# Layer 1's queries by head: two of the four masked copies moved from ScalarE to GpSimd

## The chip, the cores and the metric

The kernel runs on one core of a Trainium2 chip, in one launch. The metric is the device time of a run in microseconds (us). The engines are called as in the profile: PE is TensorE's matmul, PEld its weight load, ACT is ScalarE, DVE is VectorE, POOL is GpSimd, SP is SyncE. Times inside a run are counted from the start of the profiled span.

## The reference, cut to what matters

Four layers work on x of shape 4 x 1024 x 128. Each has a modulated layer norm, an attention, a second norm and a feed-forward part. The change lies in layer 1's attention alone, which itself has four sublayers of causal linear attention with 16 heads of 8 columns, on chunks of 128 positions:

```python
q = elu(x @ Wq[l] + bq[l]) + 1      # k likewise, v without the elu
KV = einsum('bnchd,bnche->bnhde', k, v)
KVcum = cumsum(KV, axis=1) - KV
inter = einsum('bnchd,bnhde->bnche', q, KVcum)
scores = einsum('bnchd,bnkhd->bnhck', q, k)
scores = where(tril, scores, 0.0)
intra = einsum('bnhck,bnkhe->bnche', scores, v)
out = (inter + intra) / (den_inter + den_intra + 1e-6)
x = ln(x + out @ Wo[l] + bo[l]);  y = gelu(x @ W1[l] + b1[l]) @ W2[l] + b2[l];  x = ln(x + y)
```

## The kernel before

**Stages.** Layer 0 is a program part of its own (`l0`). Layers 1 to 3 are one part (`rest`, L2056), in which some thirty chains of work run interleaved. Layer 1's attention (`l1_attn`, L892) takes the four sublayers l and the eight steps n of 128 positions (all four batches at once, so tiles are 128 x 512), which makes 32 steps.

**What sets the order.** Each chain is a Python generator. It yields requests: `run(ACT=..., POOL=...)` with a cost in us for each engine, `take(kind)` for a buffer, `wait(mark)` for another chain's mark, `rank(r)` for its precedence. The planner `Flow` (L120 to L209) keeps a clock for each engine and always goes on with the chain that can start first, or with one of lower rank that can start within 0.1 us of it. When a `run` is granted, each engine named in it has its clock set to the later of its own clock and the chain's time, plus the cost; the chain goes on at the latest of these ends. The instructions that follow in the generator are emitted at that point. PE, DVE, ACT and POOL then execute in just the emitted order (`in_order`, L483), each its own queue, and wait for each other by semaphores. The planner's costs are thus no times on the chip, but they fix the order on four engines.

**A step of layer 1.** `prep` runs in two chains, three ranks ahead. `prep_step` (L932 to L1032) makes:

- q and k: a matmul each (line L304, the helper `mm`), `min` of the biased value on DVE (L943), `relu` on ACT (L944), the exponential of both on ACT (L953), and the sum of the two on POOL (L956);
- v on DVE (L961), k transposed (PE L968, ACT L970), the running sum of k (DVE L985 to L992), and the denominator's reciprocal `rd` (DVE L1003, L1004), which POOL widens to `rde` (L1008) and PE (L1014) and ACT (L1017) turn into `rb`;
- last, **qx** and **vz**. PE works on groups of 32 rows, which hold four heads. `qx` holds q four times, the s-th copy kept only where the row belongs to the s-th head of its group: ACT multiplies q by a column of zeros and ones (L1024, four times 128 x 512). `vz` spreads v over a tile of zeros (POOL L1027, four copies). Both have two buffers. Then the mark `aprep` is set.

Around it:

- `scores` (L1039) multiplies k with qx on PE (L304, out `three` and one more bank), in two pairs of batches;
- `mask_dve` (L1066) masks three of four banks on DVE (L1073); `mask_act` (L1081) copies the fourth out on ACT (L1089) and masks it on POOL (L1093);
- `state` (L1097) makes the chunk's k v product, masked on DVE (L1116) and added up on POOL (L1122, L1124), into `kvb` and `kv`;
- `values` (L1129) multiplies q with kv and kvb (PE L1145), then vz with the masked scores (PE L1163, many small matmuls);
- `attn_out` (L1173) divides (DVE L1182) and projects (DVE L1190);
- `tail` (two chains) does the norms and the feed-forward with four gelus (ACT L1212). A norm (`norm`, L506) goes PE L514, ACT L517, DVE L523 and L525, POOL L527 and L528, DVE L531, PE L539, ACT L543 or L547.

The planner reckons a POOL operation on 512 columns at `pool_len(512)` = 0.2 + 0.0021 * 512 = 1.28 us, and one qx on ACT at 0.72 us.

## Time and profile before

| | before |
|---|---|
| median of 3 runs | 1982.12 us (1981.19 to 1982.89) |
| profiled execution, own time | 1977.38 us |
| its span in the profile | 1975.6 us |
| mean granted TensorE clock | 0.974 |
| PE, DVE, ACT, POOL busy in the span | 1802.3, 1200.7, 1033.8, 774.7 us |
| layer 1's qx: ACT L1024 | 128 instructions, 82.0 us busy |
| layer 1's vz: POOL L1027 | 128 instructions, 32.2 us busy |

The profiled execution lies 4.74 us under the median of the runs and 3.81 us under the fastest of them; 1.78 us of its own time lie outside the span. A row of busy tenths has one digit for each fortieth of the span, 49.4 us. Busy time of PE is modelled and matmuls overlap, so 92% is not the share of PE's peak. A wait is put down to the engine whose semaphore came last; "issue" says that no such release was seen within the last microsecond. In a timeline the columns are start, length, engine, line, operation, out<-in, and in brackets how long the engine stood idle before it and what ended that. A merged row such as "x4" stretches from the start of the first to the end of the last.

### The profile page before, as it was taken

Reading aid. Unit: us, or ns where it says so; the run is one execution under the profiler, and the core shown is the slowest. Engines: PE = TensorE matmul, PEld = TensorE weight load, DVE = VectorE, ACT = ScalarE, POOL = GpSimd, SP = SyncE. Lnnn points to the kernel's source line nnn. Section 1 sums busy time; section 2 is a strip of 40 time slices with the busy share of each in tenths; the row PEclk is TensorE's granted clock in tenths of the full one; section 3 lists DMA queues with packets and bytes.
Section 4 is the critical chain, followed back from the end, with each engine's and each line's share of the span. In section 5 each row is a group of like instructions: output and inputs, shape, how many; then the busy total and the mean of one; then the engine's idle time right before and its main releaser. Section 6 shows DMA issues by size and latency. Waiting matters only on the chain. (4 is left out here: it accounts for less than half of the span.)

```text
span 1975.6 us, 59172 instructions
## 1 busy us (share of the span) xinstructions
PE 1802.3 (91%) x25252; PEld 1101.9 (56%) x25252; DVE 1200.7 (61%) x3933; ACT 1033.8 (52%) x1793; POOL 774.7 (39%) x1027
## 2 busy tenths in 40 slices
PE   6999999788999999999898898999999898988896
PEld 4665444555555555555555554445555765655762
DVE  5676633555666666666666666764436766666663
ACT  4554422445555555555554545554445446558654
POOL 1344554433434443433334332454345424343421
PEclk9999999899999999999999998999999899999898
DMA  6322231000000000000000001111120000000000
GB/s 248 116 58 71 90 102 55 1 3 3 3 3 2 3 3 2 3 3 3 2 3 3 3 2 55 60 56 55 51 62 13 13 12 13 2 12 7 19 12 32
DMA packets 30615, 62.32 MB, mean 32 GB/s; under 512 B 4304, under 2 KB 6480, under 8 KB 29456
## 3 DMA queue, kind: packets, MB, share of 16 engines
q1 hardware_dynamic: 28736, 54.04, 8.6%
q8 instruction: 198, 3.24, 0.7%
q0 software_dynamic: 896, 3.16, 0.5%
q10 hardware_dynamic: 720, 1.34, 0.2%
q14 instruction: 65, 0.53, 0.1%
HBM read 56.16 MB, written 2.36 MB: 30 GB/s over the span
## 5 line engine op out<-in xcount | busy, mean ns | idle before, releaser
L304 PE MATMUL ps<-h,w 128*128 128x512 f32 x454 | 235.1, 611 | 9.3 <-DMA w<-in_g,offi 7.4
L304 PE MATMUL bank<-fu,w 128*128 128x512 f32 x456 | 221.9, 601 | 3.7 <-POOL fu L858 1.3
L527 POOL TENSOR_SCALAR ve<-mv 128x4 f32<-128x4 f32 x136 | 32.8, 241 | 375.6 <-DVE mv L525 374.1
L858 POOL TENSOR_TENSOR fu<-fu,gate 128x512 f32<-128x512 f32 x88 | 111.2, 1272 | 114.9 <-DVE fu L854 93.5
L528 POOL TENSOR_TENSOR rs<-ve,mhalf 128x4 f32<-128x4 f32 x136 | 141.5, 1040 | 11.4
L1073 DVE TENSOR_TENSOR a<-three,cst 128x1536 f32<-128x1536 f32 x64 | 112.2, 1754 | 48.0 <-PE three L304 31.9
L304 PE MATMUL acc<-h,w 128*128 128x512 f32 x266 | 137.5, 608 | 3.2 <-ACT h L547 1.6
L1093 POOL TENSOR_TENSOR a<-a,cst 128x512 f32<-128x512 f32 x64 | 82.1, 1282 | 134.1 <-ACT a L1089 134.1
L304 PEld LDWEIGHTS bank<-fu,w 128*128 128x128 f32 x456 | 80.3, 191 | 86.0 <-issue 60.9
L1303 POOL TENSOR_TENSOR fu<-fu,w 128x512 f32<-128x512 f32 x56 | 75.6, 1356 | 127.2 <-ACT fu L1299 127.0
L304 PEld LDWEIGHTS ps<-h,w 128*128 128x128 f32 x454 | 80.8, 194 | 78.3 <-issue 64.5
L304 PE MATMUL ps<-fu,w 128*128 128x512 f32 x224 | 120.8, 623 | 2.4 <-ACT fu L1717 1.6
L1163 PE MATMUL ps<-a,vz 64*32 64x64 f32 x5888 | 95.5, 225 | 21.3 <-issue 21.3
L1163 PEld LDWEIGHTS ps<-a,vz 64*32 64x32 f32 x5888 | 78.6, 105 | 46.3 <-issue 42.9
L304 PE MATMUL bank<-h,w 128*128 128x512 f32 (+1 forms) x200 | 102.4, 598 | 0.8 <-ACT h L547 0.7
L531 DVE TENSOR_SCALAR ln_sq<-ln_sq,mv,rs 128x128 f32<-128x128 f32 x184 | 79.5, 496 | 23.7 <-POOL rs L528 23.7
L531 DVE TENSOR_SCALAR ln_xc<-ln_xc,mv,rs 128x128 f32<-128x128 f32 x188 | 77.6, 477 | 21.7 <-POOL rs L528 21.6
L531 DVE TENSOR_SCALAR ln_xn<-ln_xn,mv,rs 128x128 f32<-128x128 f32 x172 | 76.5, 511 | 18.8 <-POOL rs L528 18.6
L1024 ACT ACTIVATE qx<-aq,cst 128x512 f32<-128x512 f32 x128 | 82.0, 720 | 0.0
L304 PE MATMUL acc<-y,w 128*128 128x512 f32 (+1 forms) x226 | 71.8, 441 | 7.6 <-ACT fu L1212 7.2
L304 PEld LDWEIGHTS acc<-h,w 128*128 128x128 f32 x266 | 49.2, 196 | 52.6 <-issue 45.7
L1299 ACT ACTIVATE fu<-ps,cols 128x512 f32<-128x512 f32 x66 | 45.4, 688 | 59.6 <-PE ps L304 55.8
(1467 smaller groups left out, 4436.7 us busy)
## 6 DMA issues: line engine op xcount, KB each, us to landing
w<-gd SPq DMA_DIRECT2D x56, 256.0 KB, 3.2
gate<-gd SPq DMA_DIRECT2D x32, 256.0 KB, 3.5
w<-in_w SPq DMA_DIRECT2D x7, 1024.0 KB, 12.8
gate<-gd SPq DMA_DIRECT2D x16, 224.0 KB
gate<-gd SPq DMA_DIRECT2D x16, 192.0 KB, 3.2
gate<-gd SPq DMA_DIRECT2D x16, 160.0 KB, 3.0
gate<-gd SPq DMA_DIRECT2D x16, 128.0 KB, 3.2
aq<-gd SPq DMA_DIRECT2D x8, 256.0 KB, 3.2
```

The costliest lines, as they stand in the source:

```text
L304: PE.matmul(out, lhsT, rhs, start=start, stop=stop)
L527: G.tensor_scalar(ve.t, mv.t[:, :, 1], 1e-5, None, ALU.add)
L528: G.tensor_tensor(rs.t, ve.t, mhalf, ALU.pow)
L531: V.tensor_scalar(xt[:, t, :], xt[:, t, :], mv.t[:, t, 0:1], rs.t[:, t : t + 1], ALU.subtract, ALU.mult)
L858: G.tensor_tensor(u.t, u.t, g.t, ALU.mult)
L1024: S.activation(qx.t[:, s, :, :], q, AF.Copy, scale=K("hm")[:, s : s + 1])
L1073: V.tensor_tensor(at3.t.rearrange("p d b t -> p (d b t)").rearrange("p (s q) -> p s q", q=H), three.rearrange("p (s q) -> p s q", q=H), re ...
L1093: G.tensor_tensor(at, at, rep(K("mu64"), 8), ALU.mult)
L1163: PE.matmul(nums_[c][g32[d], b, :], vz[h64[c], b, s * P + 32 * d : s * P + 32 * d + 32], at4[d][h64[c], i, s, :], start=n == 0 and c == 0 ...
L1299: S.activation(flat(u.t), pa.t, AF.Relu, bias=C("l1f_b1", 2 * e + j))
L1303: G.tensor_tensor(us[1].t, us[1].t, g.t, ALU.mult)
```

## The change

For s = 2 and 3 the masked copy of q is made by POOL's `tensor_scalar` in place of ACT's `activation` with a scale. The tiles, the operands and the column are the same. POOL's two stand ahead of the four vz copies in POOL's queue. The request to the planner changes with them: ACT 4 * 0.72 = 2.88 us becomes 1.44, POOL 4 * 0.3 = 1.2 us becomes 1.2 + 2 * 1.28 = 3.76.

```diff
@@ -1019,9 +1019,11 @@
             qx, vz = (yield from one("qx")), (yield from one("vz"))
-            yield run(ACT=4 * 0.72, POOL=4 * 0.3)
-            for s in range(4):
+            yield run(ACT=2 * 0.72, POOL=4 * 0.3 + 2 * 1.28)
+            for s in (0, 1):
                 S.activation(qx.t[:, s, :, :], q, AF.Copy, scale=K("hm")[:, s : s + 1])
+            for s in (2, 3):
+                G.tensor_scalar(qx.t[:, s, :, :], q, K("hm")[:, s : s + 1], None, ALU.mult)
             for b in range(B):
                 to = vz.t[:, b, :].rearrange("p (j r) -> p j r", r=136)[:, :, :P]
                 G.tensor_copy(
```

## The prediction

> **What bounds the kernel now.** I read the slices of the page first, then the busy time of the layer 1 stage, then PE's waits there, and last one step of the stage in order of time. The edited line runs from 375 to 1147 us (its source view, below), so only slices 8 to 24 hold it.

> ```profile
> PE   6999999788999999999898898999999898988896
> ...
> ACT  4554422445555555555554545554445446558654
> POOL 1344554433434443433334332454345424343421
> ```

> ```profile
> 476.00:1056.00 580.00, 533.58 (x11814) 334.47 (x11813) 376.11 (x955) 333.27 (x483) 227.54 (x339) 1.00 0.01 3
> ```

> The columns of the second fence are a stretch in us, its length, and the busy time of PE, PEld, DVE, ACT and POOL (then granted clock, DMA share, GB/s). In the middle of layer 1 PE is busy 92%, DVE 65%, ACT 57%, POOL 39%. Some 23 steps run there, about 25 us each, so PE is idle 2 us a step. ACT, which the change relieves, and POOL, which it loads, are both far from full. What ACT's work can give is what PE waits for it:

> ```profile
> PE ps L1163 <- issue: 21.3, 25, 2.5
> PE acc L1163 <- issue: 11.0, 13, 1.9
> PE acc L304 <- ACT fu L1212: 7.5, 10, 2.3
> PE ps L968 <- ACT y L543: 6.2, 12, 0.5
> PE ps L304 <- ACT fu L1212: 6.1, 10, 0.6
> PE acc L968 <- ACT y L543: 4.1, 8, 0.5
> ```

> These are PE's largest waits between 370 and 1175 us (total us, times, longest). 32.3 us end at no releaser, inside the runs of small matmuls of L1163; ACT's share is 13.6 us for the gelu L1212 and 10.3 us for the norm's end L543. Now one step, POOL, ACT, PE and DVE in turn:

> ```profile
> 699.33 0.61 POOL L1008 COPY rde<-ard 128x512 f32<-128x512 f32 x1 [3.79 <-DVE ard L1004]
> 699.88 1.00 POOL L1027 COPY vz<-av 128x128 f32<-128x128 f32 x4
> 703.88 0.46 POOL L1122 TENSOR_TENSOR kvb<-kvb,kv 128x128 f32<-128x128 f32 x1 [2.99 <-DVE kvb L1116]
> ...
> 707.13 1.28 POOL L1093 TENSOR_TENSOR a<-a,cst 128x512 f32<-128x512 f32 x1 [2.27 <-ACT a L1089]
> ```

> ```profile
> 702.98 0.58 ACT L1017 COPY rb<-ps 128x512 f32<-128x512 f32 x1
> 703.44 2.56 ACT L1024 ACTIVATE qx<-aq,cst 128x512 f32<-128x512 f32 x4
> 705.90 0.68 ACT L1212 ACTIVATE fu<-acc,cols 128x512 f32<-128x512 f32 x1
> 706.48 0.58 ACT L1089 COPY a<-acc 128x512 f32<-128x512 f32 x1
> ```

> ```profile
> 706.91 0.21 PE L304 MATMUL acc<-qx,ak 32*64 32x1 f32 x1
> ```

> ```profile
> 710.20 3.03 DVE L531 TENSOR_SCALAR ln_sq<-ln_sq,mv,rs 128x128 f32<-128x128 f32 x4 [1.47 <-POOL rs L528]
> ...
> 721.22 1.11 DVE L531 TENSOR_SCALAR ln_xn<-ln_xn,mv,rs 128x128 f32<-128x128 f32 x4
> ```

> Four things are to be seen. POOL, an in-order queue, reaches vz as soon as rde is done, 3.6 us before ACT reaches qx. Behind vz POOL has a hole of 2.99 us. The four qx take 2.56 us on ACT and end at 706.00; PE comes to the scores at 706.91 without having waited. And L531 took 3.03 us instead of 1.11 while POOL ran L956 (710.14 to 712.63).

> **The change, part by part.** (1) Removed: two of four qx a step on ACT. They start 0.61 us apart and two take 1.33 us, so ACT is released 2.56 - 1.33 = 1.23 us sooner in each of 32 steps, 39 us of ACT in all. Only what PE waits for behind them counts. I went back from every idle stretch of PE in the stage through releasers and queues: those with a qx behind them in the last 15 us sum to 4.0 us (at 378, 389, 405, 428, 593 and 792 us the largest, 0.3 to 1.0 each). The 0.6 us waits that recur each step for L1212 go back to DVE's L943 and L531, not to a qx. So the gain is at most 4.0 us; without 389.5 (0.5 us, the wait for qx itself) and with a part of the two long chains I take 2.5.

> (2) Added: two POOL multiplications by a column, 128x512. The same operation stands in layer 2:

> ```profile
> L1583 POOL TENSOR_SCALAR fe<-aq,l_up x3: 1578/1604/1609, 1322.8 to 1638.7; 128x512 f32<-128x512 f32 x3
> ```

> ```profile
> L1024 ACT ACTIVATE qx<-aq,cst x128: 707/716/748, 375.2 to 1146.8; 128x512 f32<-128x512 f32 x128
> ```

> (minimum, median, maximum in ns.) All eight of L1583 took 1.57 to 1.61 us; the next instruction started 1.54 us after them. Two add 3.1 us to POOL a step, 99 us in all, against 1.28 us each in the planner. In the step above POOL runs them from 699.9 to 703.0, before ACT starts its two at 703.44; vz ends at 704.0, L1122 starts at 704.0 instead of 703.88, a delay of 0.1 us. Its readers on PE (L1145) start 4.22 us after kv is done in 13 of the 32 steps, at 709.09 here; the mask L1093 ends at 708.41 and its values run at 713.64. So the hole hides the two, and without it 3.1 us would still lie inside the 4.2. Beside vz in the middle steps DVE mostly runs L943, which POOL does not lengthen (0.75 us with or without). Cost there: zero. [...]

> (3) Where the hole is missing. Step 1: vz follows L956 at 388.11, so the pair runs to 391.2, and scores that started at 389.55 start 1.7 us later; the mask behind vz moves from 389.07 to 392.2 and ends at 393.4, which the values at 392.27 need: 1.2 us more at most. Step 2: vz starts at 401.48, the mask moves from 404.79 to 405.6. Step 31: behind vz a norm's L527 at 1146.62 comes 3.1 us later, its L531 on DVE runs only at 1151.61, and rs would be ready at 1151.1: nothing. In steps 30 and 31 an L531 (1.1 us) falls beside the pair; POOL can hold it up to 3.1 us, 0 at least: I take 0.5. Sum 1.7 + 1.2 + 0.5 = 3.4.

> [...]

> (4) The planner's costs change (ACT 2.88 to 1.44, POOL 1.2 to 3.76), and the order of four engines comes from it. It believes qx and vz done 0.88 us later, so the scores can fall behind another item of PE (a 512-column matmul holds PE 0.86 us) in every step, and anything after them may be ordered anew, past 1175 us too. No view of before shows that order. From below: all of PE's waits for L1212, L543 and behind qx gone, -28 us. From above: a margin of 4.2 us used up, below, +24. I take zero, since PE has work without a gap around the scores, and keep parts of both.

> **Sum.** The profiled execution took 1977.38 us (span 1975.6). 1977.4 - 2.5 + 3.4 + 0 = 1978.3. The median of the runs is 4.74 above the profiled one: 1983.

> **Rivals.** *Faster, 1973:* the plan, with ACT freer in its densest stretch (703 to 710), orders gelu and norms so that a third of PE's 28 us of waits goes: -9. For it: ACT works without a pause from 702.4 to 709.9. Against it: the recurring waits come from DVE. *Slower, 1995:* L1122 comes to stand behind the pair and vz with the pair started only when kvb is ready. Then it is 4.1 us late (3.1 + 1.0), which leaves 0.1 of the 4.22 before L1145; if the plan also puts L1145 one item of PE earlier (0.86), PE waits 0.74 us a step. In all 32 steps that is 24 us, in half of them +12. It decides once the margin falls under 4.1 us. For it: the planner prices the pair 0.6 us too low, so its order is tighter than the chip. Against it: L1122 stands close behind the DVE result it needs, and POOL reaches the pair early. *Not what it says, 1983:* the halves aren't made at the same time, POOL is done before ACT begins, and the scores come no sooner since PE has no time for them before 706.9. That is part of the forecast.

> **How the numbers follow.** 0.2% is 4 us, about what a measurement of this kernel can tell from no change. Forecast with its third rival: 0.42, own range 1978 to 1988. Faster rival 0.26, slower rival 0.32. A small part (0.03) of the forecast lies above 1986 and counts as slower, so: faster 0.26, same 0.39, slower 0.35. The range 1970 to 1996 reaches past both rivals by a little and leaves the far ends (-28, +24) out.

> **What would show it.** Right: POOL's two at 1.55 to 1.6 us, started straight after rde and done before ACT's two; stage length within 4 us of before; PE about 92% busy; L1122 within 0.3 us of its DVE result. Wrong: PE waits for kvb or mask (slower rival), L1212 waits shrunk (faster rival), a different rhythm of the steps with PE idle by more or less than 2 us a step, or a change after 1175 us, where nothing was edited and only the plan can act.

## The result, and the profile after

| | before | after |
|---|---|---|
| median of the runs of one comparison | 1981.84 us (1981.19 to 1982.89) | 2008.25 us (2003.05 to 2018.8) |
| profiled execution, own time | 1977.38 us | 2012.3 us |
| its span | 1975.6 us | 2010.5 us |
| PE, DVE, ACT, POOL busy | 1802.3, 1200.7, 1033.8, 774.7 us | 1820.0, 1180.5, 1001.6, 876.1 us |
| mean granted clock | 0.974 | 0.954 |

The change makes the kernel slower: ratio 1.0141, interval 1.0118 to 1.0164, some 26 us. The forecast was 1983 and its range ended at 1996. Lines of the code below the edit have numbers higher by two in the changed kernel (L1163 is L1165 there).

First, did the edit do what it says? These are the slices of the page of after, answering to those shown of before:

```profile
PE   6999999788998998899898889999999898998985
...
ACT  4554422345555554645463445544444446567663
POOL 1344455545545553644363533444344423334330
```

POOL is fuller from slice 8 to 24, PE is not; ACT is a little emptier there. Tenths are too coarse for a loss of 1.4%. The edited line in its source view (minimum, median, maximum in ns), and who waited for it:

```profile
L1026 POOL TENSOR_SCALAR qx<-aq,cst x64: 1559/1574/1610, 374.4 to 1169.9; 128x512 f32<-128x512 f32 x64
...
  PE three L304: 3.2, 2
```

The 64 new instructions took 1.57 us, the price in the prediction, and PE waited for them twice, 3.2 us in all. So the loss is elsewhere. I cut both executions where POOL's first multiplication for layer 1's experts starts (L1303, in after L1305), to the whole us, and read the busy time of PE, PEld, DVE, ACT, POOL (then clock, DMA share, GB/s) on either side; before, then after:

```profile
375.00:1205.00 830.00, 748.43 (x16440) 472.35 (x16439) 533.10 (x1440) 454.45 (x665) 315.94 (x471) 0.98 0.02 5
1205.00:1976.00 771.00, 710.19 (x7500) 434.48 (x7498) 460.60 (x1746) 415.08 (x811) 297.48 (x392) 0.97 0.09 28
```

```profile
374.00:1223.00 849.00, 758.46 (x16435) 485.72 (x16436) 513.87 (x1417) 424.46 (x606) 414.49 (x539) 0.95 0.02 5
1223.00:2011.00 788.00, 718.62 (x7510) 446.10 (x7510) 460.01 (x1771) 414.16 (x812) 301.92 (x394) 0.94 0.09 27
```

These two executions lie 34.9 us apart, more than the medians. Half of that, 18 us, lies in layer 1 (from the first qx to the exact start of that multiplication 830.0 and 848.3 us), and the other half, 17 us, behind it (770.4 and 787.8), where nothing was edited. In both parts PE is busy 8 to 10 us longer with the same instructions, at a lower clock. In sum over the execution, stretches with neither PE nor PEld busy grew from 171.7 to 189.3 us, and time at half clock from 103.1 to 184.9 us. What PE waits for in layer 1 (total us, times, longest):

```profile
PE ps L1165 <- issue: 29.5, 24, 2.5
PE acc L1165 <- issue: 13.8, 15, 1.8
PE ps L304 <- ACT fu L1214: 5.1, 5, 2.1
PE acc L968 <- POOL ak L956: 4.5, 2, 2.3
```

The waits with no releaser inside the values, 32.3 us in before, are now 43.3; every other wait is small. These stops grew by 11.0 us, and all stretches of layer 1 with neither PE nor PEld busy by 8.9 (80.7 to 89.6), so the stops are all of layer 1's added idle time. The rest of its 18.3 us, 9.4, is PE busy longer, with 79.1 us at half clock in place of 36.4. One step each in order of time shows what differs. Before, then after, PE alone:

```profile
709.89 0.29 PE L1145 MATMUL ps<-aq,kvb 32*32 32x64 f32 x8
710.11 1.12 PE L304 MATMUL ps<-fu,w 128*128 128x512 f32 x2
711.17 0.26 PE L1163 MATMUL acc<-a,vz 64*32 64x64 f32 x4
...
712.58 1.12 PE L304 MATMUL ps<-fu,w 128*128 128x512 f32 x2
713.64 0.26 PE L1163 MATMUL acc<-a,vz 64*32 64x64 f32 x4
```

```profile
850.41 0.29 PE L1147 MATMUL ps<-aq,kvb 32*32 32x64 f32 x8
850.63 0.26 PE L1165 MATMUL acc<-a,vz 64*32 64x64 f32 x4
...
854.45 0.26 PE L1165 MATMUL ps<-a,vz 64*32 64x64 f32 x4 [2.09 <-issue]
...
855.66 1.12 PE L304 MATMUL ps<-fu,w 128*128 128x512 f32 x2
```

In before the two pairs of values, some 1.4 us each, are kept apart by a gelu or projection matmul of 1.1 us. In after they follow each other and the state part L1147 without a break, PE stops for 2.09 us in the middle, and the two take 5.0 us. They stand back to back in 2 of 32 steps before and in 10 after. A single pair takes 2.05 us on average in before and 1.48 undisturbed, two in a row 5.15 us on average in after. The doubled pairs are not the whole of it: single pairs take 2.19 us on average in after, and of the 11.8 us by which the values became longer in sum (136.1 and 147.9), 5.6 come with the eight more doubled steps and 6.2 with longer single pairs.

**Where PE stops.** A pair of values is 128 matmul and 128 weight-load records. The profile's page counts the packets that brought instructions, the same in both kernels:

```profile
q8 instruction: 198, 3.24, 0.7%
```

198 packets for 50,504 records of PE and PEld: 255 records a packet, 16 KB each. I counted the records up to each of the 36 stops of 0.3 us or more in the values of layer 1 of after. Where two stops lie one packet apart, 256 records lie between them seven times and 255 twice. Less 256 for each packet landed by then, 143 records are left over at 423 us, and this remainder falls steadily to 38 at 1204 us: a line of 255.1 records a packet passes within 4 records of all 36 stops. So at each of the 36 stops PE stands at the same place of a block of 256 records. Around these stops the packet starts 1.0 us (median) after PE has entered the block ahead of the stop, and PE goes on 2.24 to 2.86 us after the packet's start, median 2.41; from the entry into one block to the entry into the next 3.5 us pass (median; 2.5 to 4.9). A pair of values has the 256 records of one block and is run in 1.48 us: by an estimate from these two times, alone between two blocks it would stop PE for some 2.0 us, with a 1.06 us pair of matmuls beside it for some 0.9. The 36 stops are 0.35 to 2.5 us long, so going on from one block to the next costs PE time in the values.

**Idle time and the clock.** A stretch at half clock lasts one to five times 3.41 us in these traces, with one in each that is cut short. There are 17 in before and 26 in after, 5 and 13 of them in layer 1; in each trace their starts lie on one grid of 3.41 us, to within 2 ns. Each follows a window of 3.41 us in which PE (with PEld) was busy only in part, 19 to 66% of it in before and 15 to 80% in after. Not every such window is followed by one: of the windows of that grid at full clock, 16 more in before were busy at most 66% and 56 more in after at most 80%, with no half clock behind them. Nor is the lower clock in layer 1 shown to come from the stops in the values: of the 13 stretches in after, 4 follow a window with such a stop in it; ahead of the other 9 PE was idle for other reasons.

### The profile page after: what moved, and what is told of

Read it like the earlier page. It is cut to its first block, busy times and chain, and to the rows that moved or that the text cites. A ratio compares the mean times of both kernels' runs of the same rounds, so it can differ in the third digit from the quotient of the medians.

```text
span 2010.5 us, 59195 instructions
## 1 busy us (share of the span) xinstructions
PE 1820.0 (91%) x25252; PEld 1126.3 (56%) x25252; DVE 1180.5 (59%) x3933; ACT 1001.6 (50%) x1731; POOL 876.1 (44%) x1091
## 4 chain that ended last, share of the span: by engine, by line
PE 74%; DVE 9%; issue 5%; ACT 5%; POOL 4%; DMA 1%; ACTq 0%; DVEq 0%; POOLq 0%; SPq 0%
PE ps L304 24%; PE acc L304 17%; PE bank L304 16%; PE ps L1165 3%; PE acc L1165 2%; PE ps L539 2%; PE three L304 2%; PE ps L514 2%; POOL qx L1026 1%; DVE fe L943 1%; PE ps L1147 1%; DVE st L523 1%; PE acc L1147 1%; POOL fu L858 1%; DVE a L1075 1%
## 5 line engine op out<-in xcount | busy, mean ns | idle before, releaser
L304 PE MATMUL ps<-h,w 128*128 128x512 f32 x442 | 231.8, 616 | 12.4 <-DMA w<-in_g,offi 7.1
L527 POOL TENSOR_SCALAR ve<-mv 128x4 f32<-128x4 f32 x136 | 32.7, 241 | 374.7 <-DVE mv L525 352.8
L304 PE MATMUL bank<-fu,w 128*128 128x512 f32 x360 | 178.4, 604 | 5.3 <-DVE rm L554 1.7
L528 POOL TENSOR_TENSOR rs<-ve,mhalf 128x4 f32<-128x4 f32 x136 | 142.1, 1045 | 11.3
L304 PE MATMUL bank<-h,w 128*128 128x512 f32 (+1 forms) x264 | 135.9, 601 | 1.6 <-ACT h L543 0.9
L1305 POOL TENSOR_TENSOR fu<-fu,w 128x512 f32<-128x512 f32 x56 | 78.6, 1409 | 129.0 <-ACT fu L1301 118.3
L304 PEld LDWEIGHTS ps<-h,w 128*128 128x128 f32 x442 | 78.6, 195 | 77.7 <-issue 58.1
L1165 PE MATMUL ps<-a,vz 64*32 64x64 f32 x4608 | 91.7, 229 | 29.6 <-issue 29.5
L304 PE MATMUL acc<-fu,w 128*128 128x512 f32 x232 | 116.9, 614 | 0.6 <-DVE fu L1304 0.6
L304 PE MATMUL acc<-h,w 128*128 128x512 f32 x214 | 112.5, 618 | 2.5 <-ACT h L547 1.6
L304 PE MATMUL ps<-fu,w 128*128 128x512 f32 x192 | 100.6, 618 | 0.0
L1165 PEld LDWEIGHTS ps<-a,vz 64*32 64x32 f32 x4608 | 75.5, 107 | 43.9 <-issue 42.8
L1026 POOL TENSOR_SCALAR qx<-aq,cst 128x512 f32<-128x512 f32 x64 | 100.0, 1572 | 0.0
L304 PEld LDWEIGHTS bank<-fu,w 128*128 128x128 f32 x360 | 62.5, 191 | 63.8 <-issue 42.5
L304 PE MATMUL ps<-y,w 128*128 128x512 f32 (+1 forms) x226 | 89.7, 508 | 4.3 <-ACT fu L1214 3.3
L531 DVE TENSOR_SCALAR ln_xn<-ln_xn,mv,rs 128x128 f32<-128x128 f32 x180 | 76.7, 490 | 25.2 <-POOL rs L528 25.0
L1165 PE MATMUL acc<-a,vz 64*32 64x64 f32 x3584 | 78.3, 228 | 13.8 <-issue 13.8
L531 DVE TENSOR_SCALAR ln_sq<-ln_sq,mv,rs 128x128 f32<-128x128 f32 x184 | 70.7, 449 | 26.8 <-POOL rs L528 26.8
L1165 PEld LDWEIGHTS acc<-a,vz 64*32 64x32 f32 x3584 | 64.2, 106 | 30.1 <-issue 27.7
```

The costliest lines, as they stand in the source:

```text
L304: PE.matmul(out, lhsT, rhs, start=start, stop=stop)
L528: G.tensor_tensor(rs.t, ve.t, mhalf, ALU.pow)
L531: V.tensor_scalar(xt[:, t, :], xt[:, t, :], mv.t[:, t, 0:1], rs.t[:, t : t + 1], ALU.subtract, ALU.mult)
L1026: G.tensor_scalar(qx.t[:, s, :, :], q, K("hm")[:, s : s + 1], None, ALU.mult)
L1165: PE.matmul(nums_[c][g32[d], b, :], vz[h64[c], b, s * P + 32 * d : s * P + 32 * d + 32], at4[d][h64[c], i, s, :], start=n == 0 and c == 0 ...
L1305: G.tensor_tensor(us[1].t, us[1].t, g.t, ALU.mult)
```

## The experiments

Theory A: the planner's new costs bring an order with pairs of values back to back, and PE runs out of instructions. Theory B: POOL's 3.1 us a step hold up something (the rival of the prediction). Ratios are against runs of before on the same chip.

**1. The work without the order, the order without the work.** `work_only` keeps before's request and order and moves two qx; `plan_only` is the changed kernel with all four qx on ACT.

```diff
 # work_only, against before
-                S.activation(qx.t[:, s, :, :], q, AF.Copy, scale=K("hm")[:, s : s + 1])
+                S.activation(qx.t[:, s, :, :], q, AF.Copy, scale=K("hm")[:, s : s + 1]) if s < 2 else G.tensor_scalar(qx.t[:, s, :, :], q, K("hm")[:, s : s + 1], None, ALU.mult)
 # plan_only, against after
-            for s in (0, 1):
+            for s in range(4):
                 S.activation(qx.t[:, s, :, :], q, AF.Copy, scale=K("hm")[:, s : s + 1])
-            for s in (2, 3):
-                G.tensor_scalar(qx.t[:, s, :, :], q, K("hm")[:, s : s + 1], None, ALU.mult)
```

> The request of before (ACT 2.88, POOL 1.2), but two of the four qx on POOL. PE's and DVE's orders are those of before, line for line. Order theory and the prediction's steps 1 to 3: 1978 to 1986 us, stage of layer 1 within 4 us of 830. Theory of POOL's load: most of the loss comes with the work, 1995 to 2015.

> The planner's request of the changed kernel (ACT 1.44, POOL 3.76), but all four qx on ACT as before. PE's and DVE's orders are those of the changed kernel. Order theory: the new order alone costs the time, so 2000 to 2018 us, with the stage of layer 1 near 848 us (before 830) and the rest near 788 us (before 770). Theory of POOL's load (the two multiplications on POOL delay what stands behind them): with POOL relieved the time falls back to 1978 to 1986.

`work_only` 1986.53 us, 1.0002 (0.9985 to 1.0018). `plan_only` 2012.2 us, 1.0134 (1.0111 to 1.0156). The whole loss is the order, B falls. POOL in the step of `work_only` that the prediction worked out:

```profile
704.41 0.61 POOL L1008 COPY rde<-ard 128x512 f32<-128x512 f32 x1 [3.78 <-DVE ard L1004]
705.00 3.12 POOL L1024 TENSOR_SCALAR qx<-aq,cst 128x512 f32<-128x512 f32 x2
708.07 1.00 POOL L1027 COPY vz<-av 128x128 f32<-128x128 f32 x4
709.03 0.46 POOL L1122 TENSOR_TENSOR kvb<-kvb,kv 128x128 f32<-128x128 f32 x1
```

The pair begins behind rde and fills the hole, as forecast. In 20 of its 32 steps POOL is done before ACT begins. In after, with the new order, the two halves overlap in 27 of 32.

Before and `work_only` also give a price of the clock: they have the same order on PE and nearly the same idle time (171.7 and 172.2 us), but 103.1 and 130.2 us at half clock, and spans of 1975.6 and 1987.1. So 27 us at half clock went with 11 us, and that much lies between executions of one order (23 runs of before on this chip: 1977 to 1993). The profiled execution of before was a quick one of its order. `work_only` and `plan_only` are the fairer pair: layer 1 took 835.1 and 847.4 us, 12.3 more, of which 10.6 are the stops in the values (32.0 and 42.6); behind it 777.2 and 786.6, 9.4 more.

**2. Other costs.** `true_price` is after with the measured price of POOL's operation; `plan_064` is before with a slightly cheaper qx; `act_cost` and `pool_cost` are before with one half of the new request each.

```diff
-            yield run(ACT=2 * 0.72, POOL=4 * 0.3 + 2 * 1.28)   # after
+            yield run(ACT=2 * 0.72, POOL=4 * 0.3 + 2 * 1.58)   # true_price
-            yield run(ACT=4 * 0.72, POOL=4 * 0.3)              # before
+            yield run(ACT=4 * 0.64, POOL=4 * 0.3)              # plan_064
+            yield run(ACT=2 * 0.72, POOL=4 * 0.3)              # act_cost
+            yield run(ACT=4 * 0.72, POOL=4 * 0.3 + 2 * 1.28)   # pool_cost
```

> The changed kernel with POOL's two priced at the measured 1.58 us in place of 1.28 us in the planner. If the loss came from the planner pricing POOL too low, it goes: 1980 to 1990 us. Order theory in its general form: another order, a time anywhere in 1975 to 2020, and PE's idle and half-clock time tell which. Theory of POOL's load: as the changed kernel, 2000 to 2015.

> The kernel before with qx priced at 0.64 us in place of 0.72 us in the planner (2.56 us for four, which is what the chip takes); no instruction is moved to another engine, only the order is planned anew. Order theory: the time moves by more than 4 us either way, with no work changed. Theory of POOL's load: 1978 to 1986 us.

> The kernel before (all qx on ACT) with ACT's share of the request alone lowered to 1.44 us; POOL's stays at 1.2. In this order no two pairs of values stand back to back, and the order behind layer 1 is 75% like the changed kernel's. Theory of two losses: stage of layer 1 at 815 to 832 us (no loss there), the part behind it 780 to 790 us, total 0.998 to 1.010 of before. Rival (ACT's lower price alone is what spoils layer 1's order): stage of layer 1 840 us or more, total 1.010 to 1.020.

> The kernel before (all qx on ACT) with POOL's share of the request alone raised to 3.76 us; ACT's stays at 2.88. Two pairs back to back as before, an order behind layer 1 that is unlike either kernel's. Theory of two losses: stage of layer 1 824 to 836 us as before, the part behind open, 765 to 792 us, total 0.995 to 1.012. Rival (POOL's price alone makes the bad order in layer 1): stage of layer 1 840 us or more.

`true_price` 2010.65 us, 1.0117 (1.0094 to 1.014): a truer price gives no better order. It also shows that theory A is not all that an order can do to layer 1. Only 5 of its steps have doubled pairs, its values take 138.5 us and stop PE little more than in before (32.3 us there):

```profile
PE ps L1163 <- issue: 28.3, 26, 2.5
...
PE acc L1163 <- issue: 5.8, 6, 1.8
```

Yet its layer 1 is the longest of the re-priced kernels, 855.3 us: against before, 6.3 us more of idle time and 19.0 us of PE busy longer, with 96.1 us at half clock. What in its order brings that was not settled.

`plan_064` 1990.12, 1.0019 (1.0002 to 1.0036): it moved less than expected. `act_cost` 1995.45, 1.0026 (1.0009 to 1.0044), and `pool_cost` 1993.09, 1.0029 (1.0013 to 1.0045): neither half makes the loss by itself. Their layer 1 took 836.8 and 837.6 us, with 0 and 2 doubled pairs. For `act_cost` that lies above the 815 to 832 expected, though its stops in the values fell to 23.1 us: PE was idle 5.8 us less than in before, but busy 12.6 us longer.

**3. Pairs joined, pairs kept apart.** `before_joined` asks for both pairs in one piece. The others put a pause for the planner between the pairs, in which it gives PE to other chains (a mark that becomes due 2.0, 1.5, 1.0 or 3.0 us later; no instruction is added). The two waits that `before_joined` drops stand also at the head of the step, so nothing starts before its operands are there.

```diff
 # before_joined, against before
-                    yield wait(("dve", l, n, pair))
-                    yield wait(("act", l, n, pair))
...
-                    yield run(PE=VALUES)
+                    if not pair:
+                        yield run(PE=2 * VALUES)
 # after_apart2 (after_apart15, plan_apart15: 1.5, against after and plan_only; before_apart1, before_apart3: 1.0, 3.0, against before)
+                    if pair:
+                        fl.mark(("apart", l, n), 2.0)
+                        yield wait(("apart", l, n))
                     yield run(PE=VALUES)
```

> The kernel before (all qx on ACT), but the two pairs of values are asked of the planner as one piece (2 * 1.05 us), so that their 256 matmul records a step stand back to back on PE in all 32 steps; before they stood apart in all but 2. Theory of instruction supply (PE runs dry where some 500 of its instructions follow each other without a long matmul, since the next block of them lands only then): the runs of values take 5 us in place of twice 2.05, about +1 us a step, and with the half clock that follows idle stretches 20 to 60 us slower than before. Order theory without that cause: another order, a time anywhere within 20 us of before, values at 136 us in sum as before.

> The changed kernel (two qx on POOL, its costs), but the chain of values lets 2.0 us of planned time pass ahead of its second pair, so that the planner puts other work of PE between the pairs: no two pairs stand back to back (10 did), 1.6 to 5 us of other PE work lie between. Theory of instruction supply: values fall from 148 us to 100 to 125 us in sum, the stage of layer 1 by 15 us or more; total 10 to 35 us faster than the changed kernel, so 0.985 to 1.003 of before. Rival (the new order is bad for other reasons, such as waits for norms): values get shorter but the total stays within 6 us of the changed kernel, 1.010 to 1.017 of before.

> The kernel before with the same pause ahead of the second pair, 1.0 us of planned time: 1.7 or 2.5 us of other PE work between the pairs where before had mostly 0.9. All qx on ACT. Theory of instruction supply: values fall from 136 us to 100 to 120 us, total 10 to 25 us faster than before. Rival: another order, within 10 us of before either way.

> As the one with 1.0 us, with 3.0 us of planned time: 1.6 to 8 us of other PE work between the pairs, in a less regular order. Theory of instruction supply: values near 95 to 110 us, total 10 to 30 us faster than before unless the longer hold of the mask buffers costs more. Rival: within 15 us of before either way, slower if the mask buffers bind.

> The changed kernel with a pause of 1.5 us of planned time ahead of the second pair of values, in place of 2.0. No pairs stand back to back, and the order of PE behind layer 1's attention is nearly that of the kernel before (98% alike), where the one with 2.0 had nearly that of the changed kernel (79%). Theory (two separate losses: instruction supply in layer 1, and the other order behind it): stage of layer 1 795 to 812 us, the part behind it 768 to 778 us where the pause of 2.0 gave 786; total 0.978 to 0.987 of before, faster than with 2.0 (0.990). Rival (the part behind is slow for what layer 1 leaves behind, not for its own order): the part behind stays at 783 to 790 us, total 0.987 to 0.993.

> The same plan as the one with the pause of 1.5 us, PE's and DVE's orders line for line, but all four qx on ACT. What two qx on POOL are worth in a good order: by the prediction's step 1 at most 4 us and by the pair work_only and before nothing, so within 4 us of the other one; if ACT's relief counts once PE's instruction stalls are gone, 5 to 15 us slower than it.

| kernel | us | ratio, interval | values, us | layer 1 | behind it |
|---|---|---|---|---|---|
| before (profile) | | | 136.1 | 830.0 | 770.4 |
| after (profile) | | | 147.9 | 848.3 | 787.8 |
| before_joined | 2050.86 | 1.0376 (1.0333 to 1.0419) | 170.7 | 902.6 | 769.4 |
| after_apart2 | 1961.13 | 0.9904 (0.987 to 0.9937) | 108.4 | 802.0 | 786.3 |
| after_apart15 | 1966.07 | 0.9884 (0.9863 to 0.9906) | 117.2 | 815.3 | 776.1 |
| plan_apart15 | 1972.27 | 0.9923 (0.9902 to 0.9945) | 116.6 | 814.9 | 778.5 |
| before_apart1 | 2006.26 | 1.0145 (1.0109 to 1.0181) | 104.5 | 839.8 | 787.6 |
| before_apart3 | 1998.68 | 1.0097 (1.0063 to 1.013) | 113.2 | 848.7 | 779.5 |

Joining makes layer 1 72.6 us longer, and the whole 73, where 20 to 60 were expected; it leaves what lies behind it alone. Keeping the pairs apart in the changed kernel makes layer 1 46 us shorter than in after and beats both kernels. PE's waits in layer 1 with no releaser, `before_joined`, then `after_apart2`:

```profile
PE ps L1162 <- issue: 38.1, 23, 2.3
PE acc L1162 <- issue: 32.1, 18, 2.3
```

```profile
PE ps L1166 <- issue: 4.7, 8, 1.0
...
PE acc L1166 <- issue: 3.7, 4, 1.8
```

The waits of 32.3 us in before become 70.2 or, from 43.3 in after, 8.4. Two runs went the other way than expected: `before_apart1` and `before_apart3` do run the values faster than before, but their orders bring new waits in layer 1 (15.3 us of PE for POOL's rde and 15.1 for ACT's q in `before_apart1`), and the part behind it became 17 and 9 us longer. `after_apart15` met its forecast behind layer 1 (776.1) but not in it (815.3 where 795 to 812 was expected), and its ratio lies where the rival put it. `plan_apart15`, the same plan with all qx on ACT, is 6 us slower, where step 1 of the prediction allowed 4. A pause is a change of costs like any other: it repairs one place and draws the rest anew.

**4. Half the instructions.** The runs so far move the order. These keep it and change the number of instructions: one matmul moves the columns of both batches of a pair (128 in place of 64) over the first batch's vz, so the second batch is multiplied with the first's vz. `joined_wide` has the edit of `before_joined` besides.

```diff
-                    for i in range(2):
+                    for i in range(1):
...
-                                        nums_[c][g32[d], b, :], vz[h64[c], b, s * P + 32 * d : s * P + 32 * d + 32],
-                                        at4[d][h64[c], i, s, :], start=n == 0 and c == 0 and s == 0 and b == 0,
+                                        nums_[c][g32[d], b : b + 2, :], vz[h64[c], b, s * P + 32 * d : s * P + 32 * d + 32],
+                                        at4[d][h64[c], :, s, :], start=n == 0 and c == 0 and s == 0 and b == 0,
```

> The kernel before, but each matmul of the values moves the 64 columns of both batches of a pair at once (128 columns) over the weights of the first: as many columns moved, half the instructions, the planner's costs and so the order unchanged. The second batch of a pair gets the first's vz, so its values are not those of the reference. Theory of the instruction blocks (a block of 256 records costs PE at least some 3.5 us, and a pair of values is one block run in 1.48 us): the 32 us of waits with no releaser in the values fall under 10 us, and the time falls by 25 to 55 us, ratio 0.972 to 0.987. Rival theory, that these waits come with the arithmetic of the values themselves (their weights, columns and PSUM): the waits stay above 20 us and the time within 10 us of before.

> The changed kernel with the same half number of instructions in the values (the second batch of a pair gets the first's vz). Block theory: the waits with no releaser in the values fall from 43 us to under 10 us, and layer 1 comes within 6 us of layer 1 in before with the same edit; what is left of the change's loss is what lies behind layer 1, 10 to 20 us more than there. Rival theory: layer 1 stays about 18 us longer than in before with the same edit.

> The kernel before with the two pairs of values in one piece in every step, and half the instructions in the values (the second batch of a pair gets the first's vz). With all instructions the joining cost 73 us. Block theory: both pairs are now one block of 256 records, with half a block of small matmuls ahead of it, so PE waits at most 1 us a step for it; the time is 0 to 25 us above before with the edit of the values alone. Rival theory: most of the 73 us stays, 45 us or more above before with the edit of the values alone.

| kernel | us | ratio, interval | values, us | layer 1 | behind it |
|---|---|---|---|---|---|
| before_wide | 1922.24 | 0.97 (0.967 to 0.9731) | 75.5 | 773.0 | 775.9 |
| after_wide | 1936.25 | 0.9763 (0.9728 to 0.9798) | 76.7 | 774.8 | 787.2 |
| joined_wide | 1942.63 | 0.9806 (0.9774 to 0.9838) | 75.7 | 795.6 | 769.6 |

The waits in the values of `before_wide`, then of `after_wide`:

```profile
PE acc L1163 <- issue: 0.9, 1, 0.9
...
PE ps L1163 <- issue: 0.4, 1, 0.4
```

```profile
PE ps L1165 <- issue: 2.0, 2, 1.5
...
PE acc L1165 <- issue: 0.5, 1, 0.5
```

From 43.3 us to 2.5, and in before from 32.3 to 1.3. The changed order costs layer 1 now 1.8 us, where it cost 18.3; joining costs it 22.6 us, where it cost 72.6. With the stops at the block of instructions (36 of 36) this makes the supply of instructions the cause of the stops in the values, and so of layer 1's added idle time in after. That PE's longer busy time there (9.4 us between the profiled executions, 1.7 between `work_only` and `plan_only`) comes from it too is not shown. Two things keep the comparison from being clean. An undisturbed pair itself became shorter, from 1.48 to 1.16 us, which is 64 * 0.32 = 20 of the 60 us that `before_wide` gained (it gained more than expected). And layer 1 of `joined_wide` still takes 22.6 us more, of which PE's waits in the values are 6.9.

## Why the prediction was wrong

- **Steps 1 to 3 held.** A gain of 2.5 and a cost of 3.4 were forecast, together +0.9; `work_only` measured 1.0002, with an interval of some 3 us either way, so the two terms are confirmed as small and not one by one. The price of POOL's operation was right (1.57 us), the hole hid it in the old order, and PE waited 2.1 us for the new qx in `work_only` where 1.7 was forecast for that wait. No run shows the 0.5 in the cost, for an L531 held up beside the pair; it was picked between 0 and 3.1 us, and a hold near 3.1 is not seen. In after four L531 in a row, 1.11 us at 721.22 in before, took 1.68 us at 663.56, 867.50 and 1077.89 and 1.18 us at 1168.92, each beside a pair of 3.14 to 3.18 us.
- **Step 4 failed:** "I take zero" for the new order. The order alone cost 1.0134 in `plan_only`, 25 us by the medians. Its reason, that PE has work without a gap around the scores, looked at the scores alone; the new order made PE stop longer in the values (10.6 us more in `plan_only` than in `work_only`) and run longer behind layer 1 (9.4 us). The size of the far end, +24, was near by luck: its mechanism was another, since nothing of PE waits for kvb in after. The 0.86 us of a 512-column matmul, which the rival uses, is the planner's price (`mm_len(512)`); on the chip two of them took 1.12 us at 710.11 in before.
- **The cause stood in a view that the prediction showed.** The largest PE waits, 32.3 us, ended at no releaser inside the values. They were noted and then left out of the sum. The count of records per packet would have led to the neighbours of the values on PE: in after a doubled run takes 5.15 us where two single pairs of before take 4.1, and 5.33 in `before_joined`.
- **The planner has no such price.** It reckons a pair of values at 1.05 us of PE wherever it stands, so an order with the pairs together is as good to it as the other. All four orders that came from changed prices alone were slower than before's (`plan_only` 1.0134, `plan_064` 1.0019, `act_cost` 1.0026, `pool_cost` 1.0029); the chances, 0.26 for faster and 0.35 for slower, were nearly even.
- **Behind layer 1** the prediction named what would refute it, "a change after 1175 us, where nothing was edited and only the plan can act", and put no price on it. It cost 17 us between the profiled executions, 9.4 between `work_only` and `plan_only`.
- **The clock** was not in the sum. The loss of 34.9 us between the profiled executions is 17.6 us with neither PE nor PEld busy and 17.3 us of their being busy longer with the same work.

**What stays open.** Behind layer 1 the kernels fall mainly into two kinds: some 769 to 778 us with 60 us of idle PE (before, `work_only`, `before_joined`, `plan_064`, `after_apart15`), and 781 to 788 us with 65 to 70 (after, `plan_only`, `after_apart2`, `before_apart1`, `act_cost`). Executions of one order differ by 7 us there (before and `work_only`), so the idle time tells the kinds apart better than the length. `after_wide` keeps the loss there (787.2 against 775.9), so it does not come from the stops in the values. In after the idle time is spread over many waits of 1 to 4 us for DVE and ACT, with none that recurs; which property of the order makes them was not settled. Nor was why `plan_apart15` is 6 us over `after_apart15`, with intervals that just touch.

## What to carry to other kernels

Where a planner sets the order, an edited cost is a change of order everywhere behind it: run the new order with the old work and the old order with the new work before arguing about either. The waits of PE that end at no releaser inside the long runs of small matmuls were no background here: 32.3 us in before, 8.4 in `after_apart2` with other work between the runs, 1.3 in `before_wide` with fewer, wider matmuls. Count the records per instruction packet (255 here) where such waits stand. Read the granted clock beside the idle time of PE: from before to `before_joined` 48.2 us more of idle came with a span 71.2 us longer, from `before_wide` to `joined_wide` 18.5 us with 15.2, so idle time has no fixed price here.
